# A two-layer graph network with a mixture of experts: the all-rows expert's weights in the root weights' place, bf16 graph biases, layer-two root rows from SBUF

## The chip, the cores and the metric

The kernel runs on one core of a Trainium2 chip. The metric is the device time of one execution in microseconds (us), as the median of repeated runs. Engines are named as in the profile: PE (TensorE matmul) and PEld (its weight loads), DVE (VectorE), ACT (ScalarE), POOL (GpSimd), SP (SyncE, which issues most DMAs). POOL issues the indirect DMAs, that is, gathers and scatters by an index.

## The reference

`x` has 1250 rows of 512 floats, and there are 41,250 edges `src -> dst`, sorted by `dst`, one self loop for each row among them. Two graph convolutions, a residual, and an expert-choice feed-forward follow each other:

```python
def graph_conv_max(x, W_rel, b, W_root):
    agg = segment_max(x[src], dst, num_segments=1250)   # empty rows become 0
    return agg @ W_rel.T + b + x @ W_root.T
h = relu(graph_conv_max(layernorm(x), W1_rel, b1, W1_root))
h = relu(graph_conv_max(h, W2_rel, b2, W2_root))
x = x + h
z = layernorm(x)
probs = softmax(z @ Wr, axis=0)                 # 8 experts, over the 1250 rows
vals, idx = top_k(probs.T, 512)                 # every expert takes its 512 best rows
hid = gelu(einsum('ecd,edf->ecf', z[idx], W1) + b1e[:, None])
out = x + scatter_add(vals[..., None] * (einsum('ecf,efd->ecd', hid, W2) + b2e[:, None]), idx)
```

The weights of a convolution are 512 x 512; an expert's are 512 x 256 and 256 x 512.

## The kernel before, in words

The rows lie in ten tiles of 125. Nearly every engine call goes through a small class, `InOrder`, that keeps each engine's instructions in the order in which the program issues them; the profile therefore shows all of them at line 34, and groups are told apart by the tiles' names. No scheduler moves anything: the order of the code is the order of every engine's list, and an instruction that has to wait holds what stands behind it on its engine.

**Prologue** (to about 87 us). Rows are normalized, written to a table in HBM (`table_d`) and split into three bf16 parts (`xh`). From the sorted edges, for every row, the kernel finds which source rows it needs. Of each block of 125 source rows, the two first ones of a row are taken by one-hot matmuls on PE; further ones, up to seven, by gathers of fixed size (`nat_i`, "own"); the rest goes to an overflow table: POOL scatters it row by row (`rest_d`, ten indirect DMAs), SP reads it back in another order, and `late_list` (L565) makes the indices `late_i` of it on DVE. Rows come in order of their overflow's length, so that few gathers cover all.

**First phase** of a layer (`first_phase`, L612). There are 100 block steps (`block_steps`, L582): six bf16 one-hot matmuls fill one of two PSUM buffers `pq`, then, for the first block of a tile, ACT copies it to an SBUF tile (`acc2`, shown as `acc` in the profile), and for the nine others DVE takes the maximum into it. In among the steps, at due counts, come gather groups (four gathers of 125 rows by POOL into `hb`, then DVE maxima into `wide`), and pieces of the *root part* (`root_part`, L314): for each tile, four transposes of its rows (`ahead`, loaded back from `table_d` three tiles ahead, L302), an ACT copy to `turn`, a bias matmul (a row of ones times `brow`, fp32, contraction length 1, L325) that opens the accumulation in `pm`, four fp32 matmuls with `wroot`, an ACT copy to a buffer `line`, and a store to `root_d`. In layer one `lead` is 6: six block steps are issued, then the first late lists and the first gathers of `late_i`.

**Second phase** (`second_phase`, L723). The last own gathers, the overflow results scattered back by a gather (`backs`), and for each pair of tiles the convolution: transposes of `acc`, eight fp32 matmul records with `wrel`, and the root part read back from `root_d` and added by a matmul with the identity. In layer one `hidden` (L696) applies relu into a `line` buffer, stores it to `table_d[1]` and splits it again. In layer two `residual` (L704) adds `x`, normalizes, stores `y_d`, transposes to `yT` and makes the router's logits (`Routing.logits`, L1267). `load_root` (L197) loads `wroot` and `brow`, for layer two in the middle of second phase one (`begun`, L794).

**The all-rows expert.** Expert 0 is computed on all 1250 rows, in three groups of tiles (cuts 0, 4, 7, 10), as a generator `dense_steps` (L1285) that yields twice per chunk. `begin(n)` advances it by n while fewer than four chunks wait for their gelu; `begin(4)` stands ahead of the convolutions of tiles 8 and 9, together with `constants` (L1228), which issues the loads of this expert's weights into the one-hots' old space. After the last logits `softmax` (L1321) computes the probabilities and the waiting gelus.

**Routing** (`expert_choice`, L1346). A search over eight bit groups finds each expert's threshold: each turn is one DVE count, one PE matmul over the partitions (`pn`), and small DVE work (`step_i`). At turn 0, ten PE transposes of the probabilities with ten ACT copies to `pcol` are issued behind the count's matmul; at the other turns `beside` advances the all-rows expert. Before the search, the experts' bias `fb` is split into three bf16 parts `bp` by four ACT copies and two POOL subtractions (L1402 to L1407). Then seven experts follow, each with 512 gathered rows.

Of the kernel before, what the change touches and what calls it, by code (L numbers as in the profile page):

```python
# [18 lines left out]
P = 128  # L19
# [22 lines left out]
def fast_gnn(tc, ctx, sh, io, y_d):  # L42
# [153 lines left out]

    def load_root(layer):  # L197
        wroot = gw.tile([P, KC, D], F32, name="wroot", bufs=1)
        sp.dma_start(wroot, io[f"w{layer + 1}_root_t"].rearrange("(c p) n -> p c n", p=P))
        brow = gw.tile([1, D], F32, name="brow", bufs=1)  # L200
        sp.dma_start(brow, io[f"b{layer + 1}"])
        weights[layer][:2] = wroot, brow
# [111 lines left out]
    def root_part(layer, t):  # L314

        wr, br, _ = weights[layer]
        hT = gk.tile([P, KC, TN], F32, name="turn", bufs=3)
        turned(rows_ahead.pop(t)[:TN], hT)
        if t + 3 < NT:
            fetch_row(layer, t + 3)  # L320
        else:
            fetch_root(layer, t + 3 - NT)
        yield
        pm = ps_m.tile([P, D], F32, name="pm")
        pe.matmul(pm[:TN], ones_row[:, :TN], br, start=True, stop=False)  # L325
        yield
        for c in range(KC):
            pe.matmul(pm[:TN], hT[:, c, :], wr[:, c, :], start=False, stop=(c == KC - 1))
            yield
        rt = gk.tile([P, D], F32, name="line", bufs=LINES)  # L330
        act.copy(rt[:TN], pm[:TN])
        sp.dma_start(root_d[layer][t * TN:(t + 1) * TN, :], rt[:TN])
# [217 lines left out]
    onehots(1)  # L550

# [144 lines left out]
    def hidden(t, pm):  # L696
        row = gk.tile([P, D], F32, name="line", bufs=LINES)
        act.activation(row[:TN], pm[:TN], AF.Relu)
        stored(table_d[1][t * BR:t * BR + BN, :], row)
        fetch_root(0, t + 3)  # L700
        r1 = gk.tile([P, D], F32, name="line", bufs=LINES)
        yield from parts(t, row[:TN], r1[:TN])
# [20 lines left out]
    def second_phase(layer, finish, beside):  # L723
# [52 lines left out]
        ready = (8, 9)  # L776
        if layer == 1:
            head.constants()
            head.begin(4)
        ended(8, 9)  # L780
        while going:
            on()
            if layer == 1:
                head.begin(1)
# [15 lines left out]
    for t in range(3):  # L800
        fetch_row(1, t)
    first_phase(1, 10, late_groups(1) + own_groups(1, range(EARLY)), set(range(NT)), blocks, ready_steps)

    head = Routing(tc, sh, ohs.rearrange("p t n -> p (t n)").bitcast(F32)[:, KC * N:],
                   xh.rearrange("p t k d -> p (t k d)").bitcast(F32), yT)
    head.wide = lambda: ps_q.tile([P, R, D], F32, name="pq")
    x_tiles = [head.left[:, k * D:(k + 1) * D] for k in range(6)]
# [7 lines left out]
    second_phase(1, residual, lambda: None)  # L815
# [353 lines left out]
class Routing:  # L1169
# [4 lines left out]
    def __init__(self, tc, sh, spare, spare2, yT):  # L1174
# [10 lines left out]
        def take(n, dtype=F32, of=spare):  # L1185
# [8 lines left out]
        self.prob = take(N)  # L1194
        self.tops = take(NT)
        self.sm = take(4)
        self.alike = take(P)
# [10 lines left out]
        self.dense = [(take(KC * F).rearrange("p (c f) -> p c f", c=KC),  # L1208
                       take(FC * D).rearrange("p (c d) -> p c d", c=FC)) for e in range(DENSE)]

        self.left = spare[:, self.taken:]
# [4 lines left out]
        self.waiting = []  # L1216
        self.steps = self.dense_steps()
        sp.dma_start(self.wr_s, sh["wr"].rearrange("(c p) e -> p c e", p=P))

    @staticmethod  # L1220
    def words(sh):
# [3 lines left out]
        return (KC * E + KC * P + N + NT + 4 + P + E + 9 + 2 * CC + 3 * P // 2 + NT * E * 5 // 2 + E * FC  # L1225
                + DENSE * (KC * F + FC * D)), FC * N + DENSE * NT * D

    def constants(self):  # L1228
        dve, act, pe, pool, sp = self.engines
        fw1, fw2 = self.sh["fw1"], self.sh["fw2"]  # L1230
        E, R = fw1.shape[0], self.R
        NT = len(self.sh["rows"])
        sp.dma_start(self.fb1_s, self.sh["fb1_t"])
        for e, (w1, w2) in enumerate(self.dense):
            sp.dma_start(w1, fw1[e].rearrange("(c p) f -> p c f", p=P))
            sp.dma_start(w2, fw2[e].rearrange("(c p) d -> p c d", p=P))
# [30 lines left out]
    def logits(self, t, pl):  # L1267
# [7 lines left out]
        for c in range(KC):  # L1275
            pe.matmul(pl[:, :r], self.wr_rep[:, c].rearrange("p e r -> p (e r)"),
                      self.yT[:, c, t * TN:t * TN + r], start=(c == 0), stop=(c == KC - 1))
        act.copy(self.prob[:, t * TN:t * TN + r], pl[:, :r])
# [6 lines left out]
    def dense_steps(self):  # L1285
# [6 lines left out]
        for e in range(DENSE):  # L1292
            w1, w2 = self.dense[e]
            for n, (t0, t1) in enumerate(zip(cuts, cuts[1:])):
                c0, w = t0 * TN, sum(rows[t0:t1])
                early = e == 0 and n < 2
                if early:
                    both = self.wide()
                for f in range(FC):
                    ph = both[:, f, :] if early else self.bank()  # L1300
# [20 lines left out]
    def softmax(self):  # L1321
# [9 lines left out]
        self.begin(8)  # L1331
# [3 lines left out]
    def begin(self, n):  # L1335

        for _ in range(n):
            if len(self.waiting) < 2 * self.FC:
# [7 lines left out]
def expert_choice(tc, ctx, sh, xs, yT, y_d, out, head):  # L1346
# [30 lines left out]
    mid = rp.tile([P, D], BF16, name="mid")  # L1377
# [24 lines left out]
    act.copy(bp[:B3], fb[:B3])  # L1402
    pool.tensor_sub(fb[:B3], fb[:B3], bp[:B3])
    act.copy(bp[32:64], fb[32:64])
    act.copy(mid[64:B3], fb[64:B3])
    pool.tensor_sub(fb[64:B3], fb[64:B3], mid[64:B3])
    act.copy(bp[64:B3], fb[64:B3])  # L1407
# [12 lines left out]
    for i, shift in enumerate(SHIFTS):  # L1420
# [7 lines left out]
        if i == 0:  # L1428

            for t in range(NT):  # L1430
# [4 lines left out]
        else:  # L1435
# [195 lines left out]
def gnn_expert_choice_kernel(  # L1631
# [49 lines left out]
    with tc.For_i(0, n_again, 1):  # L1681
        with ExitStack() as st:
# [3 lines left out]
            first, second = (spool.tile([P, n], F32, name=f"spare{k}") for k, n in enumerate(Routing.words(both)))  # L1686
            head = Routing(tc, both, first, second, yT)
            head.constants()
            with tc.tile_pool(name="lps", bufs=2, space=PSUM) as lps:
                for t in range(len(both["rows"])):  # L1690
                    head.logits(t, lps.tile([P, D], F32, name="pl"))
                head.wide = lambda: lps.tile([P, 2, D], F32, name="pw")
# [50 lines left out]
```

## Time and profile before

| | |
|---|---|
| median of 8 runs | 988.68 us (980.72 to 997.76) |
| the profiled execution | 990.3 us, of it 988.5 us span |
| mean granted PE clock in it | 0.901 |
| PE busy | 736.9 us (75%), 2554 instructions |
| DVE busy | 630.0 us (64%), 1154 |
| ACT busy | 158.7 us (16%), 283 |
| POOL busy | 511.9 us (52%), 535 |
| DMA | 170.57 MB, mean 173 GB/s |
| first phase of layer one | about 87 to 342 us |
| second phase of layer one | about 342 to 428 us |
| first phase of layer two | about 428 to 672 us |
| second phase of layer two | about 663 to 790 us |
| search and lists | about 790 to 832 us |
| seven experts | about 832 to 972 us, some 20 each |

A line of the timeline gives start, duration, engine, line, operation, `out<-in` with the shape of one partition by elements, how many instructions were merged, and in brackets how long the engine had been idle and what ended that wait. A line of a table by stretches gives the stretch, its length, and for PE, PEld, DVE, ACT and POOL the busy time and the number of instructions, then the granted PE clock, the DMA engines' busy share and GB/s. The stages' bounds are read from the timeline. All stages overlap at their ends, as each engine goes on by its own list.

### The profile page before, as it was taken

The numbers are of one execution on the slowest core, as the hardware profiler recorded it, in microseconds if no ns is written. First come the engines' busy times: TensorE is split into PE (matmuls) and PEld (weight loads), VectorE is DVE, ScalarE is ACT, GpSimd is POOL, SyncE is SP. The second block draws the span as 40 slices with busy tenths as digits, with TensorE's granted clock in tenths as the row PEclk, the third lists the DMA queues.
The fourth block names the chain that finished last, engine by engine and source line by source line (L and its number), as shares of the span: only waits on it lengthen the run. The fifth ranks groups of instructions, "written<-read, shape, count | busy, mean of one in ns | idle before, by whom it ended". The sixth has DMA issues, their size and how long they took to land. (4 is left out here: it accounts for less than half of the span.)

```text
span 988.5 us, 8453 instructions
## 1 busy us (share of the span) xinstructions
PE 736.9 (75%) x2554; PEld 385.4 (39%) x2554; DVE 630.0 (64%) x1154; ACT 158.7 (16%) x283; POOL 511.9 (52%) x535
## 2 busy tenths in 40 slices
PE   0294577988979685877886889787666858899992
PEld 0142233544545342434443445343333534444441
DVE  6798587988968762725985989597534366322311
ACT  0641000000101021310000000001121342211210
POOL 6434776674636476043775667477720111355642
PEclk9996789999989887889997999797977979899996
DMA  7485569676647487444786686577852132587763
GB/s 198 132 261 168 147 188 170 200 219 195 187 148 222 148 241 217 135 155 134 170 251 180 205 265 205 173 199 218 256 186 82 44 128 74 151 177 169 146 112 46
DMA packets 70377, 170.57 MB, mean 173 GB/s; under 512 B 13015, under 2 KB 17685, under 8 KB 70323
## 3 DMA queue, kind: packets, MB, share of 16 engines
q0 software_dynamic: 37472, 114.19, 43.5%
q1 hardware_dynamic: 32030, 54.66, 17.7%
q10 hardware_dynamic: 820, 1.10, 0.5%
q8 instruction: 22, 0.36, 0.2%
q14 instruction: 33, 0.26, 0.1%
HBM read 141.46 MB, written 28.40 MB: 172 GB/s over the span
## 5 line engine op out<-in xcount | busy, mean ns | idle before, releaser
L34 PE MATMUL pq<-xh,ohs 126*125 126x512 bf16 x1200 | 307.8, 402 | 92.3 <-DVE acc L34 70.7
L34 POOL DMA_INDIRECT hb<-table_d,late_i x214 | 223.8, 1046 | 166.1 <-DVE wide L34 64.2
L34 DVE TENSOR_TENSOR acc<-acc,pq 125x1024 f32<-125x1024 f32 x180 | 219.2, 1218 | 95.5 <-remote 39.8
L34 PEld LDWEIGHTS <-ohs 126*125 126x125 bf16 (+1 forms) x1221 | 171.5, 143 | 253.2 <-issue 184.1
L34 POOL DMA_INDIRECT hb<-table_d,nat_i x140 | 143.2, 1023 | 79.7 <-issue 39.6
L34 PE MATMUL pm<-wrel,turn 128*125 128x512 f32 x160 | 84.1, 674 | 17.9 <-issue 7.2
L34 PE MATMUL pm<-wroot,turn 128*125 128x512 f32 x160 | 91.0, 652 | 0.0
L34 ACT COPY acc<-pq 125x1024 f32<-125x1024 f32 x20 | 20.3, 1013 | 386.7 <-PE pq L34 265.0
L34 DVE TENSOR_TENSOR wide<-wide,hb 125x1024 f32<-125x1024 f32 (+1 forms) x60 | 71.3, 1189 | 1.8
L34 POOL DMA_INDIRECT ysel<-y_d,idx x28 | 27.7, 988 | 77.9 <-issue 31.9
L34 DVE TENSOR_TENSOR hb<-hb 125x1024 f32<-125x1024 f32 (+2 forms) x55 | 52.5, 954 | 14.2 <-DMA hb<-table_d,nat_i 10.2
L34 PE MATMUL pm<-yselT,w 128*128 128x512 f32 x112 | 52.6, 625 | 4.7 <-ACT yselT L34 4.7
L34 PEld LDWEIGHTS pm<-wrel,turn 128*125 128x125 f32 x160 | 32.8, 215 | 58.8 <-issue 47.9
L34 POOL DMA_INDIRECT out<-oo,idx x28 | 44.8, 1600 | 15.8 <-DVE oo L34 8.5
L34 PE MATMUL pm<-w,hT 128*128 128x512 f32 x112 | 52.7, 591 | 0.0
L34 DVE TENSOR_TENSOR wide<-hb 125x1024 f32<-125x1024 f32 (+1 forms) x40 | 47.9, 1198 | 4.2 <-issue 2.2
L34 DVE TENSOR_SCALAR oo<-pm,val 128x512 f32<-128x512 f32 x28 | 21.0, 751 | 44.0 <-PE pm L34 41.6
L34 POOL DMA_INDIRECT hb<-ovf_d,slot_i x20 | 20.8, 1042 | 36.1 <-DVE wide L34 30.6
L34 PEld LDWEIGHTS pm<-wroot,turn 128*125 128x125 f32 x160 | 33.5, 210 | 11.8 <-issue 3.3
L34 ACT COPY turn<-pt 128x500 f32<-128x500 f32 x40 | 22.8, 574 | 93.0 <-PE pt L34 49.4
L34 PE MATMUL pt<-ident,acc 125*128 125x125 f32 x80 | 14.1, 316 | 29.8 <-ACT ohs L34 14.8
L34 DVE COPY got<-pi 128x20 f32<-128x20 f32 x7 | 1.2, 178 | 52.3 <-PE pi L34 52.3
(236 smaller groups left out, 773.7 us busy)
## 6 DMA issues: line engine op xcount, KB each, us to landing
w<-in_fw SPq DMA_DIRECT2D x14, 512.0 KB
ohs<-idx_d SPq DMA_DIRECT2D x10, 615.2 KB
ahead<-table_d SPq DMA_DIRECT2D x20, 250.0 KB
root_d<-line SPq DMA_DIRECT2D x20, 250.0 KB
ahead<-root_d SPq DMA_DIRECT2D x20, 250.0 KB
ovf_d<-line SPq DMA_DIRECT2D x18, 224.0 KB
hb<-table_d,late_i POOLq DMA_INDIRECT x214
ohs<-in_x SPq DMA_DIRECT2D x10, 250.0 KB
```

The lines of the kernel that those rows point to most:

```text
L34: made = call(*args, **kwargs)
```

## The change: what it does

1. **Bias.** `brow` and its fp32 matmul of contraction length 1 are replaced by one bf16 matmul of contraction length 96: the bias as three bf16 parts, at partitions 0, 32 and 64 of `bias_b`, against `three`, which has ones in these rows. `load_root` zeroes a `line` buffer on POOL and loads the bias three times into it ahead of `wroot`. A new function `split_bias` makes the parts by four ACT copies and two POOL subtractions. It is called behind `onehots(1)` in layer one and behind `second_phase(0)` in layer two.
2. **Root rows of layer two** are transposed from `acc`, where `hidden` now writes the relu, and not loaded back from `table_d[1]`.
3. **Weights.** `wroot` moves to the pool that lives on; the all-rows expert's weights are loaded into its place, ahead of `backs((8, 9))` in layer two (`load_dense`).
4. **Order.** `constants` and the first products of the all-rows expert come behind the last convolutions: `begin(2)` for each turn of the loop over the last tiles. All three groups of products are made before the softmax ends; the third one in `ps_m`.
5. **Routing.** Five of the ten transposes stand at turn 1 and five at turn 2; `beside` starts at turn 3. All six instructions of the experts' bias run on POOL.

```diff
+    B3 = 96
+    bias_b = gw.tile([P, D], BF16, name="bias_b")
+    three = gw.tile([P, TN], BF16, name="three")
+    pool.memset(three[:B3], 0.0)
+    for g in range(3):
+        pool.memset(three[32 * g:32 * g + 1, :], 1.0)
     def load_root(layer):
-        wroot = gw.tile([P, KC, D], F32, name="wroot", bufs=1)
+        wroot = keep.tile([P, KC, D], F32, name="wroot")
+        bias_f = gk.tile([P, D], F32, name="line", bufs=LINES)
+        pool.memset(bias_f[:B3], 0.0)
+        for g in range(3):
+            sp.dma_start(bias_f[32 * g:32 * g + 1, :], io[f"b{layer + 1}"])
         sp.dma_start(wroot, io[f"w{layer + 1}_root_t"].rearrange("(c p) n -> p c n", p=P))
-        brow = gw.tile([1, D], F32, name="brow", bufs=1)
-        sp.dma_start(brow, io[f"b{layer + 1}"])
+    def split_bias(layer):
+        bias_f = weights[layer][1]
+        act.copy(bias_b[:B3], bias_f[:B3])
+        pool.tensor_sub(bias_f[:B3], bias_f[:B3], bias_b[:B3])
+        act.copy(bias_b[32:64], bias_f[32:64])
+        act.copy(bias_b[64:B3], bias_f[64:B3])
+        pool.tensor_sub(bias_f[64:B3], bias_f[64:B3], bias_b[64:B3])
+        act.copy(bias_b[64:B3], bias_f[64:B3])
...
     def root_part(layer, t):
-        turned(rows_ahead.pop(t)[:TN], hT)
-        if t + 3 < NT:
+        turned(rows_ahead.pop(t)[:TN] if layer == 0 else acc[:TN, t, :], hT)
+        if layer == 0 and t + 3 < NT:
             fetch_row(layer, t + 3)
...
-        pe.matmul(pm[:TN], ones_row[:, :TN], br, start=True, stop=False)
+        pe.matmul(pm[:TN], three[:B3, :], bias_b[:B3], start=True, stop=False)
...
     own_early(1)
     fetch_early(2)
     onehots(1)
+    split_bias(0)
...
     def hidden(t, pm):
-        row = gk.tile([P, D], F32, name="line", bufs=LINES)
-        act.activation(row[:TN], pm[:TN], AF.Relu)
-        stored(table_d[1][t * BR:t * BR + BN, :], row)
+        act.activation(acc[:TN, t, :], pm[:TN], AF.Relu)
+        stored(table_d[1][t * BR:t * BR + BN, :], acc[:, t, :])
...
         backs((8, 9))
         ready = (8, 9)
+        ended(8, 9)
         if layer == 1:
             head.constants()
-            head.begin(4)
-        ended(8, 9)
         while going:
             on()
             if layer == 1:
-                head.begin(1)
+                head.begin(2)
...
     second_phase(0, hidden, begun)
-    for t in range(3):
-        fetch_row(1, t)
+    split_bias(1)
...
-    head.wide = lambda: ps_q.tile([P, R, D], F32, name="pq")
+    head.wide = [wide_q, wide_q, lambda: [ps_m.tile([P, D], F32, name="pm") for f in range(2)]]
...
-    second_phase(1, residual, lambda: None)
+    head.load()
+    second_phase(1, residual, head.load_dense)
...
+    def load_dense(self):
+        sp = self.engines[4]
+        for e, (w1, w2) in enumerate(self.dense):
+            sp.dma_start(w1, self.sh["fw1"][e].rearrange("(c p) f -> p c f", p=P))
+            sp.dma_start(w2, self.sh["fw2"][e].rearrange("(c p) d -> p c d", p=P))
...
-                early = e == 0 and n < 2
+                early = e == 0
+                while early and any(t not in self.have for t in range(t0, t1)):
+                    yield
...
-        self.begin(8)
+        while len(self.waiting) < self.FC * 3:
+            next(self.steps)
...
-    act.copy(bp[:B3], fb[:B3])
+    pool.tensor_copy(bp[:B3], fb[:B3])
     pool.tensor_sub(fb[:B3], fb[:B3], bp[:B3])
-    act.copy(bp[32:64], fb[32:64])
-    act.copy(mid[64:B3], fb[64:B3])
-    pool.tensor_sub(fb[64:B3], fb[64:B3], mid[64:B3])
-    act.copy(bp[64:B3], fb[64:B3])
+    pool.tensor_copy(bp[32:64], fb[32:64])
+    pool.tensor_copy(bp[64:B3], fb[64:B3])
+    pool.tensor_sub(fb[64:B3], fb[64:B3], bp[64:B3])
+    pool.tensor_copy(bp[64:B3], fb[64:B3])
...
-        if i == 0:
-            for t in range(NT):
+        if i in (1, 2):
+            for t in range(NT // 2) if i == 1 else range(NT // 2, NT):
...
-        else:
+        elif i:
             beside()
```

## The prediction

> **What bounds the kernel now.** I read the page's busy times first, then its chain of work that ended last, then busy times by stage, and last the timeline at the places the diff touches.
>
> ```profile
> PE 736.9 (75%) x2554; PEld 385.4 (39%) x2554; DVE 630.0 (64%) x1154; ACT 158.7 (16%) x283; POOL 511.9 (52%) x535
> ...
> POOL out L34 0%; POOLq L1680 0%
> ```
>
> No engine is full, and the chain breaks off at the last scatter, so there is no one path to follow. By stages (PE and DVE busy):
>
> ```profile
> 117.00:342.00 225.00, 184.25 (x684) 101.12 (x683) 186.24 (x209) 19.27 (x28) 134.06 (x129) 0.92 0.67 187
> ...
> 437.00:672.00 235.00, 191.49 (x699) 103.51 (x698) 182.54 (x171) 18.68 (x27) 150.75 (x146) 0.91 0.69 200
> ```
>
> The columns after the length are PE, PEld, DVE, ACT and POOL. The two first phases, half the span, need PE (184, 191) and DVE (186, 183) almost equally: six matmuls fill one of two pq buffers, DVE takes its maximum, and each waits for the other. A stop of either delays both. ACT looks free at 16%, but every engine runs its list in program order, so an ACT instruction that waits holds all behind it. The start of layer one is the place that matters:
>
> ```profile
> 87.49 5.16 PE L34 MATMUL pq<-xh,ohs 126*125 126x512 bf16 x12
> ...
> 90.30 1.01 ACT L34 COPY acc<-pq 125x1024 f32<-125x1024 f32 x1 [8.08 <-PE pq L34]
> 90.40 2.00 POOL L34 DMA_INDIRECT rest_d<-wrel,slot_i  x1 [10.98 <-DVE slot_i L34]
> ...
> 95.55 1.22 DVE L34 TENSOR_TENSOR acc<-acc,pq 125x1024 f32<-125x1024 f32 x1
> ...
> 114.00 0.23 DVE L34 MAX8 lov<-wrel 125x8 f32<-125x64 f32 x1 [7.43 <-DMA wrel<-rest_d]
> ...
> 114.61 0.94 POOL L34 DMA_INDIRECT hb<-table_d,nat_i  x1 [0.30 <-issue]
> ...
> 117.18 0.94 POOL L34 DMA_INDIRECT hb<-table_d,late_i  x1 [1.63 <-DVE lov L34]
> ...
> 118.95 2.54 DVE L34 TENSOR_TENSOR acc<-acc,pq 125x1024 f32<-125x1024 f32 x2
> ...
> 120.21 2.72 PE L34 MATMUL pq<-xh,ohs 126*125 126x512 bf16 x6 [11.46 <-DVE acc L34]
> ```
>
> ACT copies block 0 at 90.30; DVE then takes blocks 1 to 5 (95.55 to 106.56) and stops until 114.00 for the overflow table that POOL scatters (ten `rest_d`, from 90.40) and SP reads back; then come the late lists, and the first late gather at 117.18. POOL has no pause from 90.40 to 115.55.
>
> **A. The first bias split (the largest term).** split_bias(0) stands after onehots(1), ahead of the block steps. In the changed kernel's instruction order ACT has four bias_b copies directly ahead of the block-0 copy, the second and the fourth waiting for a POOL subtraction. On POOL the two subtractions stand behind the ten `rest_d` scatters and seven `nat_i` gathers, and the second also waits for all eight of POOL's DMA semaphores, thus for those gathers to land. The price of the chain itself comes from the routing's bias, split in the same way:
>
> ```profile
> 796.07 0.62 ACT L34 CAST bp<-fb 96x512 bf16<-96x512 f32 x1
> ...
> 796.29 0.56 PE L34 MATMUL pn<-sat,ohs 128*128 128x1 f32 x2 [6.13 <-ACT xh L34]
> ...
> 796.76 1.15 POOL L34 TENSOR_TENSOR fb<-fb,bp 96x512 f32<-96x512 f32 x1 [5.77 <-ACT bp L34]
> ...
> 797.95 0.62 ACT L34 CAST bp<-fb 32x512 bf16<-32x512 f32 x1 [1.26 <-POOL fb L34]
> ...
> 799.33 1.15 POOL L34 TENSOR_TENSOR fb<-fb,mid 32x512 f32<-32x512 f32 x1 [1.42 <-ACT mid L34]
> ...
> 800.51 0.61 ACT L34 CAST bp<-fb 32x512 bf16<-32x512 f32 x1 [1.32 <-POOL fb L34]
> ```
>
> Unhindered the chain is 801.12 - 796.07 = 5.05 us. Here the first subtraction starts at about 115.9, after the last gather, and ends at 117; two copies follow until 118.3; the second subtraction starts there, or when the gathers have landed. Two copies later (0.61 and 1.01) the block-0 copy ends between 121.4 and 122.9, instead of at 91.3.
>
> Queued behind it: PE has filled both pq buffers and cannot make block 2; DVE cannot take block 1, and behind that stand blocks 2 to 5 and the late lists; POOL waits for those lists. Before, DVE's stop until 114.00 was spent with blocks 1 to 5 done; now the readback is long there, and the blocks come after it. From the block-0 copy to the end of block 5 took 106.56 - 91.3 = 15.3 us, of which 3.1 was a wait for `ahead` that is now over: 12.2 to 15.3, so 134 to 138. The late lists then take 118.95 - 114.00 = 4.95, and DVE's next block maximum starts at 139 to 143 instead of 118.95: +20 to +24. POOL's first late gather, 3.2 us into the lists, falls at 137 to 141 instead of 117.18: +20 to +24. Against that, PE passes its idle 11.46 us to earlier pieces and the first gathers wait ready in their buffers, so a few us can be caught up. I take +19.5, bounds +14 and +24. All three busy engines are shifted together, and the stage that follows has no stop long enough to hide it.
>
> [...] If a ready copy could pass a waiting one, the term would be 0 and the sum about 981. The rows of this trace show no instruction out of its listed order.
>
> **B. The second bias split and the layer boundary.** Gone: ten loads `ahead<-table_d`, and the wait that PE has for the first.
>
> ```profile
> 433.94 1.06 PE L34 MATMUL pt<-ident,ahead 125*128 125x125 f32 x4 [5.26 <-DMA ahead<-table_d]
> 434.94 2.07 PE L34 MATMUL pm<-brow,ones_row 1*125 1x512 f32 x2
> ```
>
> ACT is free at 431.16; 5.05 later bias_b is ready, at 436.2, and the bias matmul, then the wroot ones at about 437.0, where they begin at 436.93 now. The stall only changes its name: 0 to +2, I take +1. POOL's two subtractions stand ahead of the late gathers, which start some 4.5 us later; a POOL idle of 12.16 us before 463.06 covers it. Without that cover it would cost 4.5.
>
> **C. Twenty bias matmuls on PE.** A pair of K=1 fp32 records moves the next matmul by 461.35 - 460.30 = 1.05 us; the routing's bf16 96x512 matmul moves it by 0.24 (815.39 to 815.63). 20 x 0.8 = 16 us of PE time at most. But DVE is as busy as PE in these stages: in the waits from 428 to 660 PE waited 27.5 us for DVE, DVE 16.2 for PE. Only where DVE waits can the gain reach the end: about a quarter, -4.5, bounds 0 and -16.
>
> **DMA.** 10 x 250 KB = 2.5 of 170.57 MB is not moved, at DMA shares of 0.67 to 0.69 in the first phases: 0 to -5 (5 being the one measured wait for such a load), I take -1. New: three 2 KB loads (SP issue 0.31 each) and four POOL memsets (about 1.1) in the prologue, hidden by POOL's 4.73 us idle there; without it +1.
>
> **D. Tail.** Now PE waits 7.23 us for the dense expert's weights, asked for at 750.57, then works cold:
>
> ```profile
> 755.25 10.00 PE L34 MATMUL pq<-ohs 128*128 128x500 f32 x16 [7.23 <-DMA ohs<-in_fw]
> ...
> 804.45 0.43 PE L34 MATMUL pn<-sat,ohs 128*128 128x1 f32 x2
> ...
> 804.91 0.16 DVE L34 TENSOR_SCALAR step_i<-pn 128x1 int32<-128x1 f32 x1 [4.35 <-PE pn L34]
> ```
>
> The weights come earlier, in wroot's place, and the four chunks (10.00 us) go behind convolutions 8 and 9. Those begin when the backs are merged (755.98) and start cold: the logits would be 7.0 us earlier, but begin(2), eight matmul records, now comes between them. Warm weight loads from 761.73 to 764.67 follow every 0.42 us, so eight records take 3.4, and 2.5 at 375 columns: 3.4 twice and 2.5 put logits 9 some 2 us earlier. Of the dense work 24 narrow records, 7.5 us, remain, until about 794.4, so the first search matmul comes at 794.5 for 796.29. The second search step stands at 804.91 behind ten transposes that ACT's bias copies held up; with the copies on POOL and the transposes five and five later, it is 6.6 earlier, of which the transposes' new places (two steps of about 2.8 in place of 2.6) and one cold dense piece (+1.5 to +3) take back some: end of search -5, bounds 0 and -7. Seven experts follow unchanged at some 20 us each, so this reaches the end whole.
>
> **Sum.** 990.3 (profiled) + 19.5 + 1 - 4.5 - 1 - 5 = 1000.3. The profiled run stands 1.6 above the median of 988.7, so 998.7: I predict 999.
>
> **Rivals.**
> 1. Not slower: in both first phases PE and not DVE sets the pace, so that all 16 us of C come off. 987. It decides from C = 14.5, where C and the rest just cancel A. For it: PE's busy time is the largest (191 against 183 in layer two). Against: PE waits longer for DVE than DVE for PE.
> 2. The block is caught up: waits for gathers in the stage 87 to 342 (DVE "remote" 14.2 us) vanish because PE and DVE come late. 999 - 14 = 985. Against: those gathers follow the same late lists.
> 3. The tail gives nothing, as begin(2) holds every logit: 1004. For it: PE idles there only 7.23 us in one piece; against: 4.35 us at 804.91 is a wait of its own.
> 4. A is longer: POOL's gathers land later, PE restarts cold (0.43 a matmul at 87.49 for 0.24 warm) and loses its place to DMA: A = 24 to 28, 1007.
>
> That the loads removed in B were hidden anyway is half my case already: only the first was waited for.
>
> **Chances.** My forecast 0.50, within 993 to 1006; rival 1 0.15, 2 0.13, 3 0.10, 4 0.12. A measurement of this kernel tells about 1% from no change: faster is below 978.8, slower above 998.6. Faster: a third of rivals 1 and 2, 0.10. Same: the rest of these, 0.18, and 0.22 of my forecast and rival 3, 0.40. Slower 0.50. The range 983 to 1010 leaves out half of rivals 1 and 2 and the top of rival 4.
>
> **What would show it.** Right: in the changed trace the first ACT copy acc<-pq ends near 122 with a wait for POOL or bias copies before it, PE idles about 25 us from 92, the first `late_i` gather is near 138, and the first phase ends some 15 to 20 us later; no `brow` rows; the bias matmul near 436; logits 9 about 2 us and the second step_i about 6 us earlier against the stage's start. Wrong: a block-0 copy at 91, a late gather before 125, or a first phase in layer two shorter by over 8 us.

## The result, and the profile after

The changed kernel takes 995.03 us (median of 22 runs, 984.6 to 1010.41) beside 984.28 us of the kernel before (64 runs): a ratio of 1.0106, 95% interval 1.0079 to 1.0133, or 10.4 us slower. The forecast was 999 from a sum of +10 us. The profiled executions have spans of 999.2 and 988.5 us, 10.7 apart, so the two traces can be laid side by side. Every ratio in this document is taken over each kernel's faster runs alone (those within 1.5% of its fastest), so it can differ from the quotient of the two medians.

The page's busy times and the busy times by stage of the changed kernel (columns as before):

```profile
PE 720.4 (72%) x2534; PEld 384.4 (38%) x2534; DVE 629.2 (63%) x1154; ACT 160.8 (16%) x287; POOL 518.4 (52%) x549
```

```profile
87.00:117.00 30.00, 4.35 (x15) 2.57 (x14) 6.96 (x14) 1.23 (x2) 20.97 (x18) 0.56 0.50 138
117.00:342.00 225.00, 179.07 (x670) 101.26 (x670) 181.18 (x216) 20.79 (x30) 127.46 (x122) 0.90 0.62 174
...
437.00:672.00 235.00, 179.72 (x672) 100.39 (x671) 170.75 (x160) 25.71 (x39) 141.69 (x139) 0.92 0.62 180
```

PE does 16.5 us less work and the kernel is slower all the same. From 87 to 117 us PE was busy for 18.65 us before, and is for 4.35 now; DVE falls from 17.63 to 6.96. Only POOL goes on as it did (20.28, now 20.97). The timeline of the changed kernel there:

```profile
80.74 0.61 ACT L34 CAST bias_b<-line 96x512 bf16<-96x512 f32 x1
...
86.10 4.16 PE L34 MATMUL pq<-xh,ohs 126*125 126x512 bf16 x12
...
89.00 2.00 POOL L34 DMA_INDIRECT rest_d<-wrel,slot_i  x1 [10.97 <-DVE slot_i L34]
...
112.74 0.95 POOL L34 DMA_INDIRECT hb<-table_d,nat_i  x1 [0.30 <-issue]
113.72 1.16 POOL L34 TENSOR_TENSOR line<-line,bias_b 96x512 f32<-96x512 f32 x1
114.91 1.24 ACT L34 CAST bias_b<-line 32x512 bf16<-32x512 f32 x2 [33.56 <-POOL line L34]
118.97 1.14 POOL L34 TENSOR_TENSOR line<-line,bias_b 32x512 f32<-32x512 f32 x1 [4.09 <-issue]
120.14 0.61 ACT L34 CAST bias_b<-line 32x512 bf16<-32x512 f32 x1 [3.99 <-POOL line L34]
120.78 1.01 ACT L34 COPY acc<-pq 125x1024 f32<-125x1024 f32 x1
...
121.83 1.22 DVE L34 TENSOR_TENSOR acc<-acc,pq 125x1024 f32<-125x1024 f32 x1 [27.59 <-ACT acc L34]
121.84 5.02 PE L34 MATMUL pq<-xh,ohs 126*125 126x512 bf16 x12 [24.95 <-ACT acc L34]
...
135.37 0.97 POOL L34 DMA_INDIRECT hb<-table_d,late_i  x1 [15.26 <-DVE lnew L34]
```

Read it from the brackets. PE fills both pq buffers from 86.10 on, transposes a tile of rows that has come by then, and from 96.89 waits 24.95 us for ACT's copy; DVE waits 27.59 for the same copy. ACT has not been working: it waited 33.56 us for a 1.16 us subtraction that stands on POOL behind ten scatters and seven gathers. The second subtraction starts 4.09 us after the end of the first. Of these, 1.3 are two copies of ACT (until 116.15); for the rest the profile names no cause (`issue`). The core's DMA traffic ends at 118.0 and the subtraction starts 1 us later, which fits the landing of those gathers, as the prediction has it, but does not show it; nor does a run show the semaphores that the prediction names. The first late gather is at 135.37 instead of 117.18.

The boundary between the layers, again in the changed kernel's timeline. Before, PE waited 5.26 us for a load at this place:

```profile
447.69 0.61 ACT L34 CAST bias_b<-line 96x512 bf16<-96x512 f32 x1
...
452.11 0.61 ACT L34 CAST bias_b<-line 32x512 bf16<-32x512 f32 x1 [1.31 <-POOL line L34]
452.35 0.96 POOL L34 DMA_INDIRECT hb<-table_d,late_i  x1 [0.27 <-POOL line L34]
...
452.78 0.58 PE L34 MATMUL pm<-bias_b,three 96*125 96x512 bf16 x1 [7.05 <-ACT bias_b L34]
453.38 2.07 PE L34 MATMUL pm<-wroot,turn 128*125 128x512 f32 x2
```

The chain of copies and subtractions takes 447.69 to 452.72, 5.03 us, and PE waits 7.05 us for its end. From the last relu of the hidden rows to the first wroot matmul it is 453.38 - 444.04 = 9.34 us, and it was 436.93 - 427.42 = 9.51. The stall has another name and the same length.

In the tail (the changed kernel's timeline), the second step of the search no longer waits:

```profile
811.46 0.34 PE L34 MATMUL pn<-sat,ohs 128*128 128x1 f32 x2
...
814.00 0.38 PE L34 MATMUL pn<-sat,ohs 128*128 128x1 f32 x2 [2.19 <-DVE sat L34]
...
814.42 0.16 DVE L34 TENSOR_SCALAR step_i<-pn 128x1 int32<-128x1 f32 x1 [0.34 <-PE pn L34]
```

The first two steps are 2.6 us apart (811.84 and 814.42), where they were 8.0 (796.89 and 804.91).

How far the changed kernel is behind, mark by mark (us, from the two timelines):

| mark | before | after | behind by |
|---|---|---|---|
| first scatter of rest_d | 90.40 | 89.00 | -1.4 |
| first late gather, layer one | 117.18 | 135.37 | 18.2 |
| block 0 of the last tile | 316.35 | 334.23 | 17.9 |
| last convolution of layer one | 422.92 | 439.54 | 16.6 |
| first convolution of layer two | 679.53 | 696.80 | 17.3 |
| convolution of tile 7 | 742.14 | 758.82 | 16.7 |
| table load of the softmax | 789.98 | 805.14 | 15.2 |
| second step of the search | 804.91 | 814.42 | 9.5 |
| last step of the search | 820.71 | 831.27 | 10.6 |
| last scatter to out | 971.95 | 982.54 | 10.6 |

One step up by 19.6 (from -1.4 to 18.2), six hundred microseconds in which 1.5 us are caught up, and one step down in the tail. The row of the last tile, as the timelines have it, before and after:

```profile
316.35 1.01 ACT L34 COPY acc<-pq 125x1024 f32<-125x1024 f32 x1 [16.55 <-issue]
```

```profile
334.23 1.02 ACT L34 COPY acc<-pq 125x1024 f32<-125x1024 f32 x1 [15.83 <-PE pq L34]
```

Between the marks the distance moves more than from mark to mark: at the first copies of tiles 4 and 8 of layer two it is 11.5 us (531.11 and 542.58) and 22.0 us (620.95 and 642.99). A microsecond or two between marks is therefore not read as the effect of one part.

### The profile page after: what moved, and what is told of

It is laid out like the page before. It is cut to its first block, busy times and chain, and to the rows that moved or that the text cites. A ratio compares the mean times of both kernels' runs of the same rounds, so it can differ in the third digit from the quotient of the medians.

```text
span 999.2 us, 8412 instructions
## 1 busy us (share of the span) xinstructions
PE 720.4 (72%) x2534; PEld 384.4 (38%) x2534; DVE 629.2 (63%) x1154; ACT 160.8 (16%) x287; POOL 518.4 (52%) x549
## 5 line engine op out<-in xcount | busy, mean ns | idle before, releaser
L34 PEld LDWEIGHTS <-ohs 126*125 126x125 bf16 (+1 forms) x1221 | 173.8, 144 | 276.6 <-issue 206.7
L34 PE MATMUL pm<-wrel,turn 128*125 128x512 f32 x160 | 86.5, 691 | 30.3 <-ACT turn L34 26.9
L34 PE MATMUL pt<-ident,acc 125*128 125x125 f32 x120 | 20.9, 310 | 24.6 <-DVE acc L34 21.8
L34 ACT COPY turn<-pt 128x500 f32<-128x500 f32 x40 | 22.9, 574 | 91.3 <-PE pt L34 38.6
L34 PEld LDWEIGHTS pm<-yselT,w 128*128 128x128 f32 x112 | 21.6, 198 | 31.4 <-issue 24.9
```

The source lines that it names most:

```text
L34: made = call(*args, **kwargs)
```

## The experiments

In this section "before" is always the kernel before as run beside the kernel in question. Its time is not the same in all of them: 922 us down to the routing alone, 985 for the experts' bias alone and the two kernels behind it, and 973 in the last. Ratios are therefore compared, not times. None of the kernels leaves any part of the computation out.

**Layer one's split early.** POOL and ACT have gaps ahead of the prologue's list loop (5.12 us before 48.13 and 5.61 before 45.89 in the kernel before).

```diff
+    split_bias(0)
     for t0 in range(0, NT, TB):
         listed(t0, min(t0 + TB, NT))
...
     onehots(1)
-    split_bias(0)
```

> The changed kernel with one edit: layer one's bias split stands ahead of the list loop of the prologue (where POOL and ACT have gaps), not behind onehots(1). Theory (the split's place in ACT's and POOL's queues costs some 19 us, all carried to the end): the block-0 copy is back near 90 us, the first late gather near 117, and the time is 17 to 20 us below the changed kernel, about 8 us below the kernel before, ratio 0.990 to 0.993. Rival (the loss comes from the layer boundary, the second phases or the tail, and the late start would be caught up anyway): within 5 us of the changed kernel, ratio near 1.006 to 1.011.

Measured: 907.0 us beside 922.03, ratio 0.9847 (0.9831 to 0.9864). Its timeline:

```profile
86.23 1.01 ACT L34 COPY acc<-pq 125x1024 f32<-125x1024 f32 x1 [7.19 <-PE pq L34]
...
112.72 0.94 POOL L34 DMA_INDIRECT hb<-table_d,late_i  x1 [1.42 <-DVE lov L34]
```

The block-0 copy and the late gather are back where they were, and the kernel is faster than before. The theory holds; the gain against the kernel before is larger than expected (15 us for 8); how much of it is the split's place, the changed kernel's own time beside the kernel before at 922 us says, two experiments below.

**The subtractions on DVE, nothing moved.** The four ACT copies stay ahead of the block-0 copy.

```diff
-        pool.tensor_sub(bias_f[:B3], bias_f[:B3], bias_b[:B3])
+        dve.tensor_sub(bias_f[:B3], bias_f[:B3], bias_b[:B3])
...
-        pool.tensor_sub(bias_f[64:B3], bias_f[64:B3], bias_b[64:B3])
+        dve.tensor_sub(bias_f[64:B3], bias_f[64:B3], bias_b[64:B3])
```

> The changed kernel with both splits left in their places, but the four subtractions on DVE in place of POOL. It tells POOL's queue from the four extra copies on ACT. Theory (POOL's queue of seventeen indirect DMAs is what holds ACT): ACT's copies wait only for two DVE subtractions behind own_early(1), the block-0 copy ends near 98 us in place of 121.8, DVE's work until 106 shifts by some 6 us into its 7.4 us wait for the readback, so the time is 15 to 20 us below the changed kernel, ratio 0.990 to 0.996. Rival (any bias split at this place, by its length on ACT, delays the start): at most 5 us below the changed kernel.

Measured: 903.05 us beside 922.03, ratio 0.9799 (0.9781 to 0.9818). Its timeline:

```profile
90.04 0.67 DVE L34 TENSOR_TENSOR line<-line,bias_b 96x512 f32<-96x512 f32 x1
...
92.02 0.68 DVE L34 TENSOR_TENSOR line<-line,bias_b 32x512 f32<-32x512 f32 x1 [1.31 <-ACT bias_b L34]
...
93.37 1.01 ACT L34 COPY acc<-pq 125x1024 f32<-125x1024 f32 x1
...
112.42 0.94 POOL L34 DMA_INDIRECT hb<-table_d,late_i  x1 [2.06 <-DVE lov L34]
```

Same copies, same place, same length of work on ACT: the block-0 copy is some 7 us later than with the split early and DVE's wait for the readback (5.16 us left of it) takes that up. It was POOL's queue, not the work of the split. Ten scatters and seven gathers ahead of a subtraction of 1.16 us are what the change pays for. The ratio is below the expected 0.990 to 0.996, and the run is 4 us faster than the one with the split early; why is not shown (it has only five runs, and the one profiled is the slowest of them, 908.48 us).

**The changed kernel and the kernel before again,** where the kernel before takes 922 us.

> The changed kernel itself, beside the kernel before and the next runs, on whatever chip they get: the runs with the split elsewhere were some 6% faster in absolute time, the kernel before too, so the size of the change is asked for again. Theory (a fixed wait at layer one's start): some 18 us above the same kernel with the split early, so ratio 1.003 to 1.008. Rival (the loss depends on the state of the memory and shrinks with it): ratio 0.985 to 0.995, as with the split early.

> The kernel before, for its profile beside those of the other runs. Theory: the same places of waiting as in the first profile (block 0 copied at about 90 us, a PE wait for the all-rows expert's weights near the end of second phase two, a second search step late by 4 us), with shorter first phases. Rival: another stage has become the bound.

Measured: the changed kernel 925.45 us beside 922.45, ratio 1.0032 (1.0005 to 1.0059). Against the run with the split early (0.9847) the place of the split costs 1.85% of 922, 17 us; that is the size of A here. Its first late gather is 20.4 us behind that of the kernel before:

```profile
131.77 0.97 POOL L34 DMA_INDIRECT hb<-table_d,late_i  x1 [15.48 <-DVE lnew L34]
```

The change as a whole loses less here because more is won back: by the first convolution of layer two 10.0 us of it are gone, where the first pair of profiles has 0.9. The run with the split early wins 8.7 us over the same stretch (from 1.35 us behind to 7.4 ahead), so it is the other parts that win it; why they win so much less in the first pair is open. From there to the last scatter the later pair wins 10.9 us, the first 6.7. The timeline of the kernel before, taken with this comparison:

```profile
111.37 0.94 POOL L34 DMA_INDIRECT hb<-table_d,late_i  x1 [1.63 <-DVE lov L34]
...
403.00 1.07 PE L34 MATMUL pt<-ident,ahead 125*128 125x125 f32 x4 [5.61 <-DMA ahead<-table_d]
...
405.99 2.07 PE L34 MATMUL pm<-wroot,turn 128*125 128x512 f32 x2
...
687.63 9.31 PE L34 MATMUL pq<-ohs 128*128 128x500 f32 x16 [13.46 <-DMA ohs<-in_fw]
...
787.44 0.95 POOL L34 DMA_INDIRECT ysel<-y_d,idx  x1 [16.31 <-DVE val L34]
```

The wait for the all-rows expert's weights is 13.46 us here and 7.23 in the first profile, which is where the tail has more to win. (The line at 405.99 is for layer two's root rows and the last one for the routing, both below.)

**The bf16 biases alone,** in the kernel before, with layer one's split early.

```diff
-        pe.matmul(pm[:TN], ones_row[:, :TN], br, start=True, stop=False)
+        pe.matmul(pm[:TN], three[:B3, :], bias_b[:B3], start=True, stop=False)
...
+    split_bias(0)
     for t0 in range(0, NT, TB):
...
     second_phase(0, hidden, begun)
+    split_bias(1)
```

> The kernel before with the bf16 biases alone, layer one's split ahead of the list loop, layer two's behind second phase one; root rows of layer two still come from the table, the tail is as before. It prices the twenty bias matmuls without the late start. Theory (DVE paces the first phases as much as PE): -1 to -5 us, ratio 0.995 to 0.999. Rival (PE paces them, all the PE time comes off): -12 to -16 us, ratio 0.984 to 0.988.

Measured: 919.52 us beside 922.03, ratio 0.9987 (0.9964 to 1.0009): -3.3 to +0.8 us. Sixteen microseconds of PE work less are worth one, if anything. (The early split is in this too: in its trace the first scatter comes at 86.29, where the kernel before has it at 84.86, so the matmuls by themselves may be worth 1 to 2 us more.) Rival 1 of the prediction, which needed 14.5, falls.

**Layer two's root rows from SBUF alone.**

```diff
-        turned(rows_ahead.pop(t)[:TN], hT)
+        turned(rows_ahead.pop(t)[:TN] if layer == 0 else acc[:TN, t, :], hT)
...
-        act.activation(row[:TN], pm[:TN], AF.Relu)
+        act.activation(acc[:TN, t, :], pm[:TN], AF.Relu)
```

> The kernel before with layer two's root rows transposed from SBUF alone. Theory (ten loads less, PE's one wait of 5.3 us for the first of them gone, nothing put in its place): -3 to -6 us, ratio 0.994 to 0.997. Rival (the loads were hidden, and block steps of layer two wait for something else at that place): 0 +- 1.5 us.

Measured: 915.43 us beside 922.45, ratio 0.992 (0.9894 to 0.9947), -7 us. Its timeline at the boundary:

```profile
395.67 1.46 PE L34 MATMUL pq<-xh,ohs 126*125 126x512 bf16 x6
396.97 0.59 PE L34 MATMUL pt<-ident,acc 125*128 125x125 f32 x4
397.49 1.12 PE L34 MATMUL pm<-brow,ones_row 1*125 1x512 f32 x2
...
400.15 1.12 PE L34 MATMUL pm<-wroot,turn 128*125 128x512 f32 x2 [1.54 <-ACT turn L34]
```

PE goes from the block matmuls to the transposes without a pause and starts the wroot matmuls at 400.15, the first two records in 1.12 us, where the kernel before has them at 405.99, in 2.07 us, behind a wait of 5.61. By the first copy of the second tile it is 7.3 us ahead (410.37 for 417.71), and 7.8 at the last scatter. So this part is worth 7 us, slightly more than the 3 to 6 expected, and in the change the bias split, put at the same place, takes them.

**The tail alone** (parts 3, 4 and 5, biases and root rows as before).

```diff
-        wroot = gw.tile([P, KC, D], F32, name="wroot", bufs=1)
+        wroot = keep.tile([P, KC, D], F32, name="wroot")
...
+        ended(8, 9)
         if layer == 1:
             head.constants()
-            head.begin(4)
-        ended(8, 9)
         while going:
             on()
             if layer == 1:
-                head.begin(1)
+                head.begin(2)
...
-        if i == 0:
-            for t in range(NT):
+        if i in (1, 2):
+            for t in range(NT // 2) if i == 1 else range(NT // 2, NT):
```

> The kernel before with the parts 3, 4 and 5 of the change alone (root weights' place for the all-rows expert, the order of its products, transposes at turns 1 and 2, the experts' bias on POOL); biases and root rows as before. Theory: -5 to -7 us, ratio 0.993 to 0.995. Rival (the products between the last logits give the gain back): 0 +- 2 us.

Measured: 913.07 us beside 922.03, ratio 0.9897 (0.9876 to 0.9917), -9.5 us: more than expected, where the kernel before waits 6 us longer for the weights than in the first profile. The products between the logits do not give it back.

**The routing alone** (transposes at turns 1 and 2, experts' bias on POOL), and **the experts' bias on POOL alone**.

```diff
-    act.copy(bp[:B3], fb[:B3])
+    pool.tensor_copy(bp[:B3], fb[:B3])
...
-        if i == 0:
-            for t in range(NT):
+        if i in (1, 2):
+            for t in range(NT // 2) if i == 1 else range(NT // 2, NT):
...
-        else:
+        elif i:
             beside()
```

> The kernel before with the routing's part alone: five of the ten transposes at turn 1 and five at turn 2, the experts' bias all on POOL. Theory: the second search step comes some 5 us earlier, transposes and a later all-rows output take 1 us back: -4 us, ratio 0.995 to 0.997. Rival (what the tail gained in the run with the tail alone, 9 us, comes from the order of the all-rows products and their weights): 0 +- 1 us here.

Measured: 925.87 us beside 922.45, ratio 1.0034 (1.0012 to 1.0057). It loses, which neither the theory nor the rival had. The search is indeed earlier, its last step at 748.87 for 753.63 in the kernel before, and so is the first gather of the first expert, 761.04 for 765.80. But the second expert's first gather is at 789.84 for 787.44. The timeline of this run:

```profile
783.72 1.88 PE L34 MATMUL pm<-ohs,xh 128*125 128x512 f32 x4
784.32 0.75 DVE L34 SCALAR_TENSOR_TENSOR acc<-xh,gate,acc 125x512 f32<-125x512 f32 x1 [15.24 <-ACT xh L34]
...
787.20 1.48 DVE L34 TENSOR_TENSOR oh<-ohs,lane 128x1280 bf16<-128x1280 bf16 x1
```

Two outputs of the all-rows expert, which `beside` no longer makes in turns 1 and 2, now come behind the first expert's sixteen matmuls, and DVE's list for the second expert (`oh`) stands behind their sums: 15.24 us of waiting. In the changed kernel this is not seen: no output of the all-rows expert comes behind the first expert's matmuls in either of its profiles. In the first pair the first expert takes 22.5 us in both kernels (from its first gather to the second expert's). In the later pair it takes 23.5 us and 21.6 in the kernel before; there PE's sixteen matmuls take 9.98 us for 8.80.

The second of the two, the experts' bias alone:

```diff
-    act.copy(bp[:B3], fb[:B3])
+    pool.tensor_copy(bp[:B3], fb[:B3])
...
```

> The kernel before with the experts' bias split on POOL alone, the transposes left at turn 0. It halves the routing part. Theory (the ten copies to pcol waited for ACT's bias copies, 801.15 in the first profile): the second step comes some 3 us earlier, all of it reaches the end, since the all-rows outputs stay where they were, ratio 0.995 to 0.998. Rival (POOL's own chain then holds the all-rows outputs, which need the bias): 0 +- 1.5 us.

Measured: 982.82 us beside 984.59, ratio 0.9894 (0.9847 to 0.9941), from runs that scatter between 967.8 and 1001.6. Its timeline has the second step 4.2 us behind the first, where it was 8.0:

```profile
794.97 0.16 DVE L34 TENSOR_SCALAR step_i<-pn 128x1 int32<-128x1 f32 x1 [0.88 <-PE pn L34]
...
799.19 0.16 DVE L34 TENSOR_SCALAR step_i<-pn 128x1 int32<-128x1 f32 x1 [1.99 <-PE pn L34]
```

The ten copies did wait for ACT's bias copies, and without these the search is 2.6 us shorter (21.2 us from its first step to its last, 23.8 before). The interval of the ratio reaches from 6 to 15 us, which is more than that. But five of the twelve runs, 967.84 to 976.92 us, carry this ratio; the two medians are 1.8 us apart, less than the 2.6. Nothing else in the kernel is changed, so the time of this run says no more than that the gain is small, and the 2.6 us of the trace are its size.

**Both splits early,** and **the same with the transposes back at turn 0.** Layer two's bias and root weights are loaded ahead of second phase one:

```diff
         backs((0, 1, 2, 3))
+        if layer == 0:
+            split_bias(1)
...
+    load_root(1)
     second_phase(0, hidden, begun)
-    split_bias(1)
```

> The run with layer one's split early, and layer two's too: its bias and root weights are loaded ahead of second phase one, and split_bias(1) stands behind the first backs of that phase, so that nothing of it stands at the layer boundary. Theory (at the boundary the bias chain took the place of the wait for the root rows, which alone was worth 7 us): PE's wait of 7 us there goes, some 5 to 8 us below the run with layer one's split early, ratio 0.976 to 0.980. Rival (behind that wait stands another, the last parts of the hidden rows or the late gathers, or the split now holds the convolutions of second phase one): within 2 us of that run, ratio 0.982 to 0.987.

```diff
-        if i in (1, 2):
-            for t in range(NT // 2) if i == 1 else range(NT // 2, NT):
+        if i == 0:
+            for t in range(NT):
...
-        elif i:
+        else:
             beside()
```

> The run with both splits early, with one part of the change undone: all ten transposes of the probabilities at turn 0 again, the all-rows outputs from turn 1. Theory (the routing part alone lost 3 us because two all-rows outputs moved into the first expert, where DVE's list for the second expert stands behind their sums): the first expert is about 2 us shorter, but the second turn of the search is late again by the ten transposes, some 3 us, since no bias copies hold ACT now; together -2 to +2 us against the run with both splits early. Rival (the move of the transposes gains what it was made for): +4 to +6 us.

Measured: 986.94 and 984.92 us beside 984.59, both 0.9991 (0.9948 to 1.0033 and 1.0034). Both expectations for the first are missed: it is no gain over the kernel before. Against the changed kernel (1.0106) it is 1.15%, or 11 us, where moving layer one's split alone gave 17 at 922 us. The second one's trace has the first late gather at 119.12, so A is gone. From the last convolution of layer one to the first copy of the second tile of layer two both need 19.0 us (428.59 to 447.58 in the second), where the changed kernel needs 26.5 (439.54 to 466.00): the boundary is shorter by the 7 us that were expected.

What takes these gains is not shown. The second one's profiled execution took 975.37 us, 10 less than its median, and ends 15 us ahead of the first profile of the kernel before (956.83 for 971.95), so it cannot show where the median loses them. The first one's took 990.7 us, and there second phase one, from the first convolution to the last, takes 90.5 us (353.02 to 443.56), where the second one's takes 76.8 (351.75 to 428.59) and the changed kernel's 73.1; in it ACT stands 22.02 us before a relu at 405.18, and PE 20.34 before a convolution behind it. The profile puts ACT's wait down to "remote", that is, to nothing that it shows (see the last section). Whether these kernels would have won where the kernel before takes 922 us is open.

The transposes' place makes no clear difference to the time between the two, as the second expectation had it (-2 to +2 us). Its working was wrong, though: the search takes 18.7 us from its first step to its last with them at turn 0, and 20.1 at turns 1 and 2, but the first expert takes 22.7 us for 20.5 and not 2 us less.

**Subtractions on DVE and transposes at turn 0,** as the candidate for the best version: the edit of the second experiment and that of the last one.

> The changed kernel with the four subtractions of both splits on DVE, each split in its place, and with all ten transposes at turn 0 again and the all-rows outputs from turn 1. It is the candidate that should beat both kernels wherever it runs. Theory (the late start goes, the layer boundary and the first expert keep their order): on a chip where the kernel before takes some 922 us, ratio 0.976 to 0.981, the search a few us later and the first expert as much shorter than with the subtractions on DVE alone; on one where it takes 984, the gain in the second phases is taken by waits for gathers and loads, ratio 0.985 to 0.995. Rival (the gains depend on the chip altogether): 0.998 to 1.003 where the kernel before takes 984.

Measured: 969.17 us beside 973.40, ratio 0.9938 (0.989 to 0.9986). That is within the 0.985 to 0.995 expected where the kernel before takes 984 us. It is 0.6% faster than the kernel before (the medians are 0.4% apart), and the changed kernel is 1.1% and 0.3% slower than the kernel before in its two comparisons: by the ratios this version beats both, but it was not run beside the changed kernel, and beside the kernel before only once. Its timeline has the block-0 copy and the first late gather in their places, and its search takes 18.8 us from the first step to the last:

```profile
97.45 1.01 ACT L34 COPY acc<-pq 125x1024 f32<-125x1024 f32 x1
...
115.79 0.95 POOL L34 DMA_INDIRECT hb<-table_d,late_i  x1 [1.14 <-DVE lnew L34]
```

The largest gain measured is that of the subtractions on DVE alone, 0.9799, where the kernel before takes 922 us; the two were not run beside each other.

## Why the prediction was right, point by point

The time, its sign and its cause are as forecast: a sum of +10.0 us, and 10.7 in the spans, 10.4 by the ratio. The 999 itself is 4 us high because the kernel before, measured again, came out 4.4 us lower (984.28 over 64 runs for 988.68 over 8). The terms are less good than the sum: B, C and DMA together were to give 4.5 us and gave 1.5 (18.2 to 16.7 in the table). That is made up by a start 1.4 us earlier, for which there is no term, and by 1.1 us more from D. That these cancel to within 1 us is luck.

- **A, taken at +19.5 (14 to 24): right in size, by a working that was wrong in part.** From the first scatter to the first late gather the step is 19.6 us in the first pair of profiles and 19.1 in the later one; the run with the split early gives 17. The block-0 copy was to end between 121.4 and 122.9 and ends at 121.79, but two misses cancel in this: the first subtraction starts at 113.72 and not at 115.9, and the second waits longer than the copies. The first late gather was to come at 137 to 141 and comes at 135.37, because blocks 1 to 5 were to take 12.2 to 15.3 us and take 131.79 - 121.79 = 10.0. The 15.3 were misread: in the first 4.2 of them (91.3 to 95.55) DVE did other work, which in the changed kernel is done by 94.2, during the wait; the five blocks by themselves took 106.56 - 95.55 = 11.0. The lists take 4.9, as said. That a few us are caught up at once was the reason for taking 19.5 and not 20 to 24; the traces show nothing caught up at this place, and the shorter blocks in its stead.
- **That A reaches the end** is shown by experiment where the kernel before takes 922 us: with the split early or with its subtractions on DVE the first late gather is back (112.72 and 112.42) and 17 us and more are gained. Where it takes 984 us, as in the forecast, it is read from the one pair of profiles; there no kernel has layer one's split alone moved, and the two with both splits early gain 11 us on the changed kernel, less than A.
- **That an engine takes its list in order, the premise of A,** is seen for ACT in the changed kernel's trace: PE's matmuls of blocks 0 and 1 run from 86.10 to 90.26, and ACT's copy of block 0 starts at 120.78, behind the four bias copies, the second and fourth of which waited 33.56 and 3.99 us for POOL. (The 981 given in the prediction for a term of 0 counts from the profiled execution; on the scale of the 999 it is 979.)
- **B, +1 (0 to +2): right.** 9.34 us for 9.51, and POOL's late gathers, 21.1 us behind by then (4.5 more than the last convolution, as forecast), cost nothing that the next mark shows. That the loads by themselves were worth 7 us was not in the prediction's sum, but it is what the sentence "the stall only changes its name" amounts to: 7 gained, 7 put back.
- **C, -4.5 (0 to -16): the mis-sized term.** Alone it measures -1.2 (-3.3 to +0.8), and in the first pair of profiles 1.6 us are given back from the first late gather to the last convolution of layer one, and none in layer two's first phase (16.6 to 17.3). That DVE waits 16.2 us in such a stage was read as room for a quarter of the saved PE time; that share was a guess, and no run shows why it is smaller.
- **DMA, -1:** not to be told from nothing in the first pair of profiles.
- **D, -5 (0 to -7): right in its places, too small.** From the convolution of tile 7 to the end of the search 16.7 - 10.6 = 6.1 us are won: 1.5 up to the softmax (predicted 2), 7.2 at the second step (predicted 6.6), of which 1.1 is given back by the transposes' new places. The tail alone gave 9.5 where the weights' wait was longer. Which of its parts 3 and 4 gives how much was not measured. The prediction carried the gain "whole" through the experts; the routing alone shows that this holds only if no output of the all-rows expert moves behind the first expert.
- **Rivals.** Rival 1 falls with the bf16 biases alone. Rival 2 (caught up) falls in the table above, where 17.9 of 18.2 us are left at the phase's last tile; in the later pair of profiles half is won back, but by the other parts, which win 8.7 us over the same stretch without A as well. Rival 3 falls with the tail alone. Rival 4 did not come: A stayed at 19.6, though POOL's second subtraction waited and PE did restart slowly (twelve matmuls in 5.02 us from 121.84, 0.42 each, where six take 1.46 from 126.92, 0.24 each).

## What to carry to other kernels

In a kernel whose order is fixed, ask of every instruction that is added not how long it takes but what stands ahead of it in each queue that it passes: two subtractions of 1.16 us behind seventeen indirect DMAs held three engines for 25 to 34 us, and the same two on another engine did not delay the first late gather (112.42, with the split early 112.72). When a wait is removed and a chain is put at the same place, measure the two apart; here each was worth 7 us and the sum was nothing. Work removed from an engine that takes turns with another was not worth its busy time here: 16 us of PE were worth about one, and even a quarter, guessed from the waits, was too much.

## What the runs showed of the hardware that was not expected

- The kernel before takes 922 us in some comparisons and 973 to 985 in others. The two profiles of it differ from the prologue (first scatter at 84.86 for 90.40) to the last convolutions: from the first late gather to the last tile of layer one 187.6 us for 199.2, from the second to the last tile of layer two 172.0 for 196.2. From the convolution of tile 9 to the last scatter they do not differ: 198.9 for 198.6.
- In every profile of the slower comparisons there are waits put down to "remote", 78 to 137 us of them summed over the engines, and in none of the 922 us comparisons. Between 140 and 860 us the slower profiles have four to eight stops of 2 to 13 us in which none of PE, DVE and ACT runs, the others at most one, of 4.7 us. One such stop in the first profile of the kernel before, by the columns of the tables by stages; POOL goes on gathering in it:

```profile
526.40:531.00 4.60, 0.00 (x0) 0.00 (x0) 0.04 (x1) 0.00 (x0) 3.38 (x5) 0.81 0.79 256
```

What stops the engines there is not shown; the chip does not tell the two kinds apart (a comparison at 922 us and the one at 985 both ran on chip 1). The ratio of the same change to the kernel before is 1.0106 in the slower kind of comparison and 1.0032 in the other, while A is 17 to 20 us in both.

- The same subtraction of 96x512 floats takes 1.16 us on POOL (113.72 in the changed kernel) and 0.67 on DVE (90.04 in the second experiment).
